# Cross-attention block in one launch: the context copy between the relus, a third buffer for the second sum, its store ahead of the probability transfers, and the last step's normalising on ScalarE

## The chip, the core and the metric

The kernel runs on one core of a Trainium2 chip. The metric is device time in microseconds of one launch, and the median of several runs counts. Five engines work side by side, each through its own instructions in order: TensorE (PE, with its weight loads as PEld), VectorE (DVE), ScalarE (ACT), GpSimd (POOL) and SyncE (SP), which here issues nearly all transfers. They wait for one another through semaphores, and a wait holds up whatever stands behind it on the same engine.

## What is computed

One block of cross attention in float32 over 128 sequences of 128 tokens, width 256, 16 heads of 16, feed-forward width 1024:

```python
q = (x @ Wq + bq)      # 16 heads; k and v likewise from ctx
scores = q k^T / 4, kept where j < i, else -1e30
attn = softmax(scores);  attn[row 0] = 0
x1  = layer_norm(x + (attn @ v) @ Wo + bo, ln1_g, ln1_b)
out = layer_norm(x1 + relu(x1 @ W1 + b1) @ W2 + b2, ln2_g, ln2_b)
```

## The kernel before

Sequences go in pairs: pair p holds sequences 2p and 2p+1, and there are 64 pairs (`NP`). All order is written out by hand; nothing is rescheduled. The first pairs have functions of their own (`third` to `sixth`), then `step(p)` runs for p = 7 to 63, and `behind(62)`, `behind(63)` and a written-out end finish the last pairs.

A step is a software pipeline over several pairs. In `step(p)` the following happens, by engine:

- PE: `weigh(p-2)` multiplies probabilities and values into PSUM bank 7 (tile `pc`, L494 and L504), `scores_both(p)` fills all eight banks (`pss`, L384), then come the queries (`pq`, L261), `attention_out(p-2)` (`po`, L523), keys and values (`pk`, `pv`), `second_by_seven(p-4)` (the second feed-forward product by seven products instead of eight; `py` in bank 6 and `pz` in bank 7, L817) and `hidden_by_seven(p-3)` (the first feed-forward product, chunks 0 to 3 by seven products, `phs`, L907, and chunks 4 to 7 plainly, `ph`, L946). The last step uses the plain `hidden` (L718) instead.
- ACT: `context(p-2)` copies `pc` into `cxT` (L516) and so frees bank 7; then come the exponentials by head (L783), the copies of queries, keys and values, `norm1`, `norm2` of pair p-5 (L602), and the relus that make `hT` (L936 in ordinary steps, L726 where `hidden` is used). In `hidden_by_seven` the relus go in the order 4, 5, 6, 7, 0, 1, 2, 3, all before the context copy of the following step.
- POOL: `combine_hidden(p-4)` makes four sums and differences `hS` of `hT` (L803 to L806) and needs all eight relus; then `add_bo`, `combine_normed` (`xS`, L874 to L877), the small steps of the norms (`ve`, `sd`, `nb`: L543, L544, L588), the multiplication of the exponentials by one over their sums (L434), `residual1` (L577, L580) and `finish(p-5)` (L616, L617: gain and offset of the second norm on `t2`).
- DVE: masks (L398, L762) and maxima (L766, L773) of the scores, `attention_sum`, statistics (L536, L537), transposes of 32 by 32 blocks of the probabilities (`turn`, L447) and of the normed rows (`tbx`, L682), the sum `t2` of `sum_of_seven(p-4)` (L846, L854), and the additions inside `hidden_by_seven` (L919 to L931).
- SP: `turn_x1` sends the normed rows through DRAM (L239, L242), `bring(p)` carries the transposed probabilities to their partitions (`pT`, L462, 16 transfers), `store(p-5)` writes the result (L625), `load_ahead` fetches inputs (L92, L99).

The tile `t2` lives from `sum_of_seven(p-4)` in one step to `store(p-5)` in the next; its pool `ffn` has two buffers, so a new `t2` waits until the store of the second-last one has read its buffer. In `step` the order on SP is `bring(p)` and then `store(p-5)`.

In the last step (p = 63) the normalising of pair 58 is done by `norm2_by_vector` on DVE (L610), the statistics of pair 59 close the step, and half of the probability transfers of pair 63 are issued by ACT in `behind(62)`.

Of the kernel before, what the change touches and what calls it, by code (L numbers as in the profile page):

```python
# [19 lines left out]
def tile_cross_attention_block(  # L20
# [346 lines left out]
    def scores_both(p):  # L367

        st = states[p]
        for hi in range(2):  # L370
            st["sps", hi] = [
                at_bank(r if hi else (6, 7, 4, 5)[r], f"pss{hi}_{p}_{r}") for r in range(NS)
            ]
            room(p, hi)
        one, two = (0, 1), (2, 3)
        for strips, hi, m in (
            (two, 0, 0), (one, 1, 0), (two, 0, 1), (one, 1, 1),
            (two, 1, 0), (two, 1, 1), (one, 0, 0), (one, 0, 1),
        ):
            n = P if hi else HP  # L380
            for s in range(2):
                for r in strips:
                    strip, first = slice(32 * r, 32 * r + 32), s * P
                    nc.tensor.matmul(  # L384
                        st["sps", hi][r][
                            s * HP : (s + 1) * HP, m * 2 * n : (m + 1) * 2 * n
                        ].rearrange("p (e j) -> p e j", e=2),
                        st["qT"][strip, m, first + hi * HP : first + hi * HP + HP],
                        st["kT"][strip, m, :, first : first + n],
                        start=True, stop=True,  # L390
                    )
# [49 lines left out]
    def turn(p, hi, t):  # L441

        st = states[p]
        if "tb" not in st:
            st["tb"] = wide(f"tb_{p}").rearrange("p (j n) -> p j n", j=NS)
        at = (t if hi else 2) * 256
        nc.vector.transpose(  # L447
            st["tb"][:, :, at : at + 256].rearrange("p j (n a) -> p n j a", a=32),
            st["sm", hi].rearrange("p h j -> p (h j)")[:, t * 1024 : (t + 1) * 1024].rearrange(
                "p (n j a) -> p n j a", j=NS, a=32  # L450
            ),
        )
# [61 lines left out]
    def context(p):  # L514
        pc = states[p].pop("pc").rearrange("p (u i) -> p u i", i=P)
        nc.scalar.copy(cxT.rearrange("p m s i -> p (m s) i")[:, :, 1:], pc[:, :, 1:])  # L516
# [75 lines left out]
    def scale_and_shift(p):  # L592

        st = states[p]
        deviation(p, 2)
        shift(p, 2)
# [6 lines left out]
                t2[:, s], t2[:, s], AF.Identity, bias=nb[:, s], scale=sd[:, s]  # L603
            )

    def norm2_by_vector(p):
        st = states[p]
        t2, mv, sd = st["t2"], st["mv", 2], st["sd", 2]
        for s in range(2):
            nc.vector.tensor_scalar(  # L610
                t2[:, s], t2[:, s], mv[:, s, 0:1], sd[:, s], ALU.subtract, ALU.mult
            )

    def finish(p):
        t2 = states[p]["t2"]
        nc.gpsimd.tensor_tensor(t2, t2, g2_r[:, None, :].to_broadcast([P, 2, D]), ALU.mult)  # L616
        nc.gpsimd.tensor_tensor(t2, t2, be2_r[:, None, :].to_broadcast([P, 2, D]), ALU.add)  # L617
# [126 lines left out]

    def second_sum(p):
        st = states[p]
        t2 = st["t2"] = ffn.tile([P, 2, D], F32, tag="t2", name=f"t2_{p}")
        nc.vector.tensor_tensor(
            t2, st.pop("py").rearrange("p (s d) -> p s d", s=2), st.pop("x1b"), ALU.add
        )  # L750
# [85 lines left out]
    def sum_of_seven(p):  # L836

        st = states[p]
        t2 = st["t2"] = ffn.tile([P, 2, D], F32, tag="t2", name=f"t2_{p}")
        t = t2.rearrange("p s (h d) -> p (s h) d", h=2)  # L840
        py, pz = st.pop("py"), st.pop("pz")
        x1b = st.pop("x1b").rearrange("p s (h d) -> p (s h) d", h=2)

        def add(to, of, at):
            n = to.shape[1]
            nc.vector.tensor_tensor(  # L846
                to, of, py[:, None, at * P : (at + 1) * P].to_broadcast([P, n, P]), ALU.add
            )

        add(t, x1b, 0)  # L850
        add(t[:, 1:], t[:, 1:], 1)
        add(t[:, 2:], t[:, 2:], 2)
        add(t[:, 1::2], t[:, 1::2], 3)
        nc.vector.tensor_tensor(  # L854
            t[:, :3], t[:, :3], pz[:, : 3 * P].rearrange("p (n d) -> p n d", d=P), ALU.add
        )
# [95 lines left out]
    def second_half(p, s):  # L952

        st = states[p]
        py = at_bank(6, f"py_{p}_{s}")
        for f in range(FC):
            nc.tensor.matmul(
                py[:, :D], st["hT"][:, f, s * P : (s + 1) * P], w2[:, f, :],
                start=(f == 0), stop=(f == FC - 1),
            )  # L960
        if s == 0:
            st["t2"] = ffn.tile([P, 2, D], F32, tag="t2", name=f"t2_{p}")
        nc.vector.tensor_tensor(st["t2"][:, s], py[:, :D], st["x1b"][:, s], ALU.add)

    warm = bank("warm")
# [365 lines left out]
    def hidden_by_seven(p):  # L1331

        h = Hidden(p - 3)
        h.run(1)
        h.run(6)
        h.keep()
        stack_values(p)
        h.u2()
        h.run(7)
        h.run(4)  # L1340
        h.u3()
        h.run(2)
        h.run(3)
        h.run(5)
        h.rest()
        norm2(p - 5)
        h.plain([4], 0)
        h.relu(4)
        h.plain([5], 1)
        h.relu(5)  # L1350
        h.plain([6], 2)
        h.relu(6)
        turn(p, 1, 1)
        h.plain([7], 0)
        h.relu(7)
        for f in range(2 * NI):
            h.relu(f)

    def step(p):
        last = p == NP - 1  # L1360
        weigh(p - 2)
        context(p - 2)
        scores_both(p)
        combine_hidden(p - 4, POOL_ALONE)
        add_bo(p - 1)
        if not last:
            combine_normed(p - 3)
            load_ahead(p)
        mask(p, 0, B)
        if last:  # L1370
            mask(p, 0, A)
        mask_high(p, A)
        exponential_by_head(p, 1, ONES, True)
        mask_high(p, B)
        exponential_by_head(p, 1, TWOS, True)
        if not last:
            mask(p, 0, A)
        low_maximum(p)
        if not last:
            exponential_by_head(p, 0, range(H), True)  # L1380
            queries(p + 1)
        attention_out(p - 2)
        attention_sum(p - 2)
        attention_stats(p - 2)
        shift(p - 2, 1)
        if last:
            values(p)
            values_out(p)
            stats(p - 5, states[p - 5]["t2"], 2)
            deviation(p - 5, 2)  # L1390
            norm1(p - 2)
            exponential_by_head(p, 0, range(H), True)
        else:
            norm1(p - 2)
            keys(p + 1)
            values(p)
        sums(p, 1, ONE)
        sums(p, 1, TWO)
        if p + 2 < NP:
            tokens(p + 2, "x")  # L1400
            tokens(p + 2, "c")
        if last:
            norm2_by_vector(p - 5)
            turn_x1(p - 2)
        else:
            stats(p - 5, states[p - 5]["t2"], 2)
            scale_and_shift(p - 5)
        turn(p, 1, 0)
        second_by_seven(p - 4)
        if not last:  # L1410
            sums(p, 0, ALL)
        residual1(p - 3)
        sum_of_seven(p - 4)
        if last:
            sums(p, 0, ALL)
        if not last:
            turn_x1(p - 2)
            spread_values(p)
            hidden_by_seven(p)
        else:  # L1420
            turn(p, 1, 1)
            hidden(p - 3, range(FC))
        turn(p, 0, 0)
        bring(p, nc.sync, LATE_FIRST[: len(EVERY) // (1 + last)])
        finish(p - 5)
        store(p - 5)
        if last:
            stats(p - 4, states[p - 4]["t2"], 2)
            scale_and_shift(p - 4)

    third()
    fourth()
# [8 lines left out]
    def behind(p):  # L1441

        weigh(p)
        context(p)
        if p == NP - 2:
            bring(p + 1, nc.scalar, LATE_FIRST[len(EVERY) // 2 :])
        combine_hidden(p - 2, VECTOR_ALONE)
        norm2(p - 3)
        finish(p - 3)
        store(p - 3)  # L1450
        second_by_seven(p - 2)
        attention_out(p)
        attention_sum(p)
        attention_stats(p)
        shift(p, 1)
        residual1(p - 1)
        sum_of_seven(p - 2)
        stats(p - 2, states[p - 2]["t2"], 2)
        scale_and_shift(p - 2)
        hidden(p - 1, range(FC), lambda f: norm1(p) if f == 0 else None)  # L1460
        turn_x1(p)
# [16 lines left out]
    store(p - 1)  # L1478

    st = states[NP - 1]  # L1480
    t2 = ffn.tile([P, 2, D], F32, tag="t2", name="t2_last")
    for s in range(2):
        py = at_bank(6 + s, f"py_last_{s}")
        for f in range(FC):
# [49 lines left out]
```

## Time and profile before

| | us |
|---|---|
| median of 3 runs | 1533.78 |
| lowest and highest run | 1531.72, 1533.82 |
| the profiled execution's own time | 1532.45 |
| its span, first to last instruction | 1529.5 |
| what lies around the span | 2.95 |

| engine | busy us | share of the span |
|---|---|---|
| PE | 1510.4 | 99% |
| PEld | 1368.7 | 89% |
| POOL | 1358.2 | 89% |
| DVE | 1294.3 | 85% |
| ACT | 1287.0 | 84% |

The mean granted clock of TensorE is 0.998 of full speed. Busy time says how full an engine is, not whether it is late: for that one asks what each engine waited for and when. In the rows of the timeline below, the first number is the start in microseconds, the second the duration, "xN" the number of instructions merged into the row, and the bracket the idle time of that engine just before and what ended it. A row with SPq or ACTq is the issuing of transfers by that engine's queue.

### The profile page before, as it was taken

To read this page: it belongs to the slowest core of one execution; us is meant where nothing else is said; L and a number is where in the kernel's file an instruction comes from. 1 tells how busy PE (TensorE), PEld (TensorE's weight loads), DVE (VectorE), ACT (ScalarE), POOL (GpSimd) and SP (SyncE) were. 2 spreads that over 40 slices of the span, in tenths; PEclk is the share of its full clock that TensorE was granted. 3 is DMA by queue.
4 is the path that set the end of the run, shared out by engine and by line. 5 is a ranking of instruction groups with operands and counts; after the bars stand their busy time and mean duration, and the time that the engine had idled before them with its cause. 6 is when DMAs were issued, how large, how long until landed. Compare 5 with 4: busy or idle time off the path is not lost.

```text
span 1529.5 us, 53568 instructions
## 1 busy us (share of the span) xinstructions
PE 1510.4 (99%) x18598; PEld 1368.7 (89%) x18598; DVE 1294.3 (85%) x2609; ACT 1287.0 (84%) x5269; POOL 1358.2 (89%) x1508
## 2 busy tenths in 40 slices
PE   8999999999999999999999999999999999999998
PEld 6788899989989989999999999999899999999987
DVE  7989788898888888888888888888888888888875
ACT  5568888988989889889889889889898898898852
POOL 7878889999999999999999999999999999999973
PEclk9999999999999999999999999999999999999999
DMA  8456656655656656656566566556565566564441
GB/s 196 91 117 149 135 136 138 136 135 135 150 132 141 136 133 140 144 138 139 129 138 145 135 138 137 135 135 151 131 141 132 137 139 148 133 141 114 107 115 49
DMA packets 415316, 204.60 MB, mean 134 GB/s; under 512 B 282449, under 2 KB 383057, under 8 KB 415057
## 3 DMA queue, kind: packets, MB, share of 16 engines
q1 hardware_dynamic: 412768, 199.34, 56.5%
q8 instruction: 158, 2.59, 0.8%
q10 hardware_dynamic: 2288, 1.85, 0.5%
q14 instruction: 102, 0.83, 0.2%
HBM read 70.26 MB, written 33.29 MB: 68 GB/s over the span
## 4 chain that ended last, share of the span: by engine, by line
PE 91%; DVE 4%; DMA 2%; POOL 1%; SPq 1%; issue 1%; ACT 1%; ACTq 0%; POOLq 0%; DVEq 0%
PE py L817 13%; PE ph L946 12%; PE phs L907 11%; PE pz L817 10%; PE pq L261 7%; PE pss L384 7%; PE po L523 7%; PE pv L301 7%; PE pk L261 7%; PE pc L504 4%; PE pc L494 2%; PE ph L718 2%; SPq L462 1%; DVE t L846 1%; POOL sm L434 1%
## 5 line engine op out<-in xcount | busy, mean ns | idle before, releaser
L783 ACT ACTIVATE sm<-pss,nmx 128x128 f32<-128x128 f32 x944 | 328.5, 404 | 107.0 <-DVE nmx L766 95.8
L434 POOL TENSOR_TENSOR sm<-sm,rs 128x1024 f32<-128x1024 f32 x192 | 362.2, 1901 | 5.6 <-DVE rs L433 5.6
L783 ACT ACTIVATE sm<-sm,nmx 128x64 f32<-128x64 f32 x944 | 313.8, 404 | 0.0
L447 DVE STREAM_TRANSPOSE tb<-sm 128x1024 f32<-128x1024 f32 x186 | 223.3, 1226 | 71.3 <-POOL sm L434 57.8
L783 ACT ACTIVATION_READ_ACCUMULATOR sm<-sm,nmx 128x1 f32 x912 | 235.5, 258 | 0.0
L783 ACT ACTIVATION_READ_ACCUMULATOR sm<-pss,nmx 128x1 f32 x912 | 222.6, 244 | 0.0
L946 PE MATMUL ph<-x1T,w 128*128 128x256 f32 x896 | 204.8, 382 | 3.3 <-DVE hT L919 3.3
L946 PEld LDWEIGHTS ph<-x1T,w 128*128 128x128 f32 x896 | 165.7, 191 | 25.8 <-DVE hT L919 3.7
L817 PE MATMUL py<-wt,hS 128*128 128x128 f32 x1440 | 170.7, 275 | 0.9 <-DVE hS L803 0.9
L817 PEld LDWEIGHTS py<-wt,hS 128*128 128x128 f32 x1440 | 165.6, 192 | 1.0 <-DVE hS L803 1.0
L766 DVE TENSOR_REDUCE nmx<-pss 128x4 f32<-128x512 f32 x236 | 150.5, 678 | 0.0
L936 ACT ACTIVATE hT<-ph,b1e_c 128x256 f32<-128x256 f32 x224 | 98.8, 465 | 44.1 <-PE ph L946 44.1
L398 DVE TENSOR_TENSOR sm<-pss,neg 128x256 f32<-128x256 f32 (+1 forms) x276 | 108.0, 433 | 32.4 <-PE pss L384 30.2
L291 ACT ACTIVATE kT<-pk,bkh,half 128x256 f32<-128x256 f32 x252 | 123.8, 610 | 4.0 <-PE pk L261 4.0
L261 PE MATMUL pq<-xT,wq 128*128 128x256 f32 x504 | 125.4, 392 | 0.0
L523 PE MATMUL po<-wo,cxT 128*128 128x256 f32 x512 | 121.3, 380 | 0.8 <-ACT cxT L516 0.8
L301 PE MATMUL pv<-wv,cT 128*128 128x256 f32 x512 | 121.0, 379 | 0.0
L261 PE MATMUL pk<-cT,wk 128*128 128x256 f32 x504 | 119.2, 379 | 0.0
L803 POOL TENSOR_TENSOR hS<-hT 128x512 f32<-128x512 f32 x57 | 72.6, 1274 | 50.4 <-ACT hT L936 50.2
L384 PE MATMUL pss<-kT,qT 32*64 32x256 f32 (+1 forms) x3840 | 112.7, 332 | 0.6 <-ACT hT L726 0.6
L523 PEld LDWEIGHTS po<-wo,cxT 128*128 128x128 f32 x512 | 96.9, 190 | 14.4 <-ACT cxT L516 1.3
L301 PEld LDWEIGHTS pv<-wv,cT 128*128 128x128 f32 x512 | 97.2, 190 | 13.2
(165 smaller groups left out, 3982.0 us busy)
## 6 DMA issues: line engine op xcount, KB each, us to landing
pT<-tb SPq DMA_DIRECT2D x976, 96.0 KB, 2.2
x1t<-tbx SPq DMA_DIRECT2D x252, 64.0 KB, 1.8
x1T<-x1t SPq DMA_DIRECT2D x63, 256.0 KB, 2.9
out_dram<-t SPq DMA_DIRECT2D x63, 256.0 KB, 2.6
xb<-in_x_dram SPq DMA_DIRECT2D x124, 128.0 KB, 3.8
cb<-in_ctx_dram SPq DMA_DIRECT2D x124, 128.0 KB, 3.9
x<-in_x_dram SPq DMA_DIRECT2D x31, 512.0 KB, 4.7
w<-in_L_xattn_W_dram SPq DMA_DIRECT2D x2, 1024.0 KB, 7.3
```

The source lines that it names most:

```text
L261: nc.tensor.matmul(ps[:, m * TP : (m + 1) * TP], w[:, k, m * P : (m + 1) * P], src[:, k, :], start=(k == 0), stop=(k == KC - 1),)
L291: nc.scalar.activation(st["kT"][:, m, e, :], pk[:, m * TP : (m + 1) * TP], AF.Identity, bias=bkh[:, m, e : e + 1], scale=half[:, e : e + 1],)
L301: nc.tensor.matmul(pv[:, s * D : (s + 1) * D], st["cT"][:, k, s * P : (s + 1) * P], wv[:, k, :], start=(k == 0), stop=(k == KC - 1),)
L384: nc.tensor.matmul(st["sps", hi][r][s * HP : (s + 1) * HP, m * 2 * n : (m + 1) * 2 * n].rearrange("p (e j) -> p e j", e=2), st["qT"][strip ...
L434: nc.gpsimd.tensor_tensor(sm[:, part, :], sm[:, part, :], rs[:, :, None].to_broadcast([P, part.stop - part.start, n]), ALU.mult,)
L447: nc.vector.transpose(st["tb"][:, :, at : at + 256].rearrange("p j (n a) -> p n j a", a=32), st["sm", hi].rearrange("p h j -> p (h j)")[:, ...
L523: nc.tensor.matmul(po[:, s * D : (s + 1) * D], cxT[:, k, s, :], wo[:, k, :], start=(k == 0), stop=(k == KC - 1),)
L766: nc.vector.tensor_reduce(st["nmx", 1][:, 4 * r : 4 * r + 4], st["sps", 1][r].rearrange("p (n j) -> p n j", j=P), AX.X, ALU.max, negate=True,)
L783: nc.scalar.activation(sm[:, h, :], src, AF.Exp, bias=nmx[:, h : h + 1], scale=1.0, **({"accum_out": st["su", hi][:, h : h + 1]} if summed ...
L817: nc.tensor.matmul(out, left(k), right(k), start=(k == 0), stop=(k == FC // 2 - 1))
L907: nc.tensor.matmul(ps[:, i * P : (i + 1) * P].rearrange("p (n a) -> p n a", a=32), left(i), right, start=True, stop=True,)
L946: nc.tensor.matmul(self.plains[f].rearrange("p (s i a) -> p s i a", s=2, a=32), w1[:, k, f * P : (f + 1) * P], self.x1T[:, :, :, k, :], st ...
```

## The change

Four things are changed; the arithmetic of the matmuls and their order on PE stay as they are.

1. `hidden_by_seven` issues the relus 0 and 1 only (after 4 to 7), and keeps the object under `states[p - 3]["rest"]`; the relus 2 and 3 are issued in the next step, behind `context`. On ACT the copy of the context so stands between relu 1 and relu 2, in the steps 8 to 63.
2. `t2` has three buffers instead of two.
3. In the steps 7 to 62 `finish(p-5)` and `store(p-5)` are written ahead of `bring(p)`, which puts the store ahead of the 16 probability transfers on SP.
4. In the last step `norm2_by_vector(58)` on DVE goes; instead `shift(58, 2)` makes `nb` on POOL, and `norm2(58)` on ACT, `finish(58)` on POOL and `store(58)` are placed in `behind(62)` after the context copy, ahead of the eight transfers that ACT issues. The statistics of pair 59 move from the end of the last step to behind `combine_hidden` in `behind(62)`.

```diff
-    def norm2_by_vector(p):
-        st = states[p]
-        t2, mv, sd = st["t2"], st["mv", 2], st["sd", 2]
-        for s in range(2):
-            nc.vector.tensor_scalar(
-                t2[:, s], t2[:, s], mv[:, s, 0:1], sd[:, s], ALU.subtract, ALU.mult
-            )
...
-        t2 = st["t2"] = ffn.tile([P, 2, D], F32, tag="t2", name=f"t2_{p}")
+        t2 = st["t2"] = ffn.tile([P, 2, D], F32, tag="t2", name=f"t2_{p}", bufs=3)
...
         h.plain([7], 0)
         h.relu(7)
-        for f in range(2 * NI):
+        for f in range(NI):
             h.relu(f)
+        states[p - 3]["rest"] = h
 
     def step(p):
         last = p == NP - 1
         weigh(p - 2)
         context(p - 2)
+        if p > 7:
+            for f in range(NI, 2 * NI):
+                states[p - 4]["rest"].relu(f)
         scores_both(p)
...
         if last:
-            norm2_by_vector(p - 5)
+            shift(p - 5, 2)
             turn_x1(p - 2)
...
         turn(p, 0, 0)
+        if not last:
+            finish(p - 5)
+            store(p - 5)
         bring(p, nc.sync, LATE_FIRST[: len(EVERY) // (1 + last)])
-        finish(p - 5)
-        store(p - 5)
-        if last:
-            stats(p - 4, states[p - 4]["t2"], 2)
-            scale_and_shift(p - 4)
...
         weigh(p)
         context(p)
         if p == NP - 2:
+            norm2(p - 4)
+            finish(p - 4)
+            store(p - 4)
             bring(p + 1, nc.scalar, LATE_FIRST[len(EVERY) // 2 :])
         combine_hidden(p - 2, VECTOR_ALONE)
+        if p == NP - 2:
+            stats(p - 3, states[p - 3]["t2"], 2)
+            scale_and_shift(p - 3)
         norm2(p - 3)
```

More of the change, by code (lines that the diff above doesn't have):

```diff
@@ L838, in sum_of_seven @@
         st = states[p]
-        t2 = st["t2"] = ffn.tile([P, 2, D], F32, tag="t2", name=f"t2_{p}")
+        t2 = st["t2"] = ffn.tile([P, 2, D], F32, tag="t2", name=f"t2_{p}", bufs=3)
         t = t2.rearrange("p s (h d) -> p (s h) d", h=2)
@@ L961, in second_half @@
         if s == 0:
-            st["t2"] = ffn.tile([P, 2, D], F32, tag="t2", name=f"t2_{p}")
+            st["t2"] = ffn.tile([P, 2, D], F32, tag="t2", name=f"t2_{p}", bufs=3)
         nc.vector.tensor_tensor(st["t2"][:, s], py[:, :D], st["x1b"][:, s], ALU.add)
@@ L1480, in tile_cross_attention_block @@
     st = states[NP - 1]
-    t2 = ffn.tile([P, 2, D], F32, tag="t2", name="t2_last")
+    t2 = ffn.tile([P, 2, D], F32, tag="t2", name="t2_last", bufs=3)
     for s in range(2):
```

## The prediction

> **What bounds the kernel now.** I read the page's busy times first, then the list of who waited for whom on PE, then the timeline at the two places that list points to, and one ordinary step.
>
> ```profile
> PE 1510.4 (99%) x18598; PEld 1368.7 (89%) x18598; DVE 1294.3 (85%) x2609; ACT 1287.0 (84%) x5269; POOL 1358.2 (89%) x1508
> ```
>
> Of a span of 1529.5 us PE is idle for 1529.5 - 1510.4 = 19 in all. A change that leaves its instructions alone can gain only where PE waits. The list of PE's waits (total, times, longest) says where that is:
>
> ```profile
> PE ph L946 <- DVE hT L919: 3.3, 1, 3.3
> ...
> PE pc L494 <- DVE t L854: 1.9, 1, 1.9
> ...
> PE ph L718 <- DMA x1T<-x1t: 1.2, 2, 0.8
> ```
>
> Each of the first two happens once, the third twice, so none belongs to the repeated step. An ordinary step begins with the product `pc`; PE's rows at two successive steps:
>
> ```profile
> 819.39 0.43 PE L494 MATMUL pc<-pT,vd 128*32 128x64 f32 x16
> ...
> 842.61 0.43 PE L494 MATMUL pc<-pT,vd 128*32 128x64 f32 x16
> ```
>
> The step is 842.61 - 819.39 = 23.22 us, and the windows view of another step shows PE busy for all of it at full clock (second row; columns: window, length, then busy time and instructions of PE, PEld, DVE, ACT, POOL, then granted clock, DMA share, GB/s):
>
> ```profile
> 188.62:192.02 3.40, 3.30 (x8) 2.52 (x8) 3.12 (x6) 0.47 (x1) 0.00 (x0) 0.50 0.31 77
> 192.26:215.48 23.22, 23.22 (x293) 21.26 (x292) 18.76 (x42) 20.71 (x88) 20.07 (x23) 1.00 0.64 148
> ```
>
> So nothing is to be had in the ordinary step. There are two places to gain: the 3.3 us early on, and the 1.9 near the end with a smaller one behind it.
>
> **Third buffer: step 8.** The early wait lies in step 8. The rows of its start, its stall and the next step's start on PE and PEld, then DVE and SP:
>
> ```profile
> 163.84 0.27 PEld L494 LDWEIGHTS pc<-pT,vd 128*32 128x32 f32 x16 [0.33 <-issue]
> ...
> 188.72 3.61 PE L946 MATMUL ph<-x1T,w 128*128 128x256 f32 x8 [3.32 <-DVE hT L919]
> ...
> 192.26 0.27 PEld L494 LDWEIGHTS pc<-pT,vd 128*32 128x32 f32 x16 [0.48 <-issue]
> ```
> ```profile
> 184.90 0.69 DVE L846 TENSOR_TENSOR t<-x1b,py 128x512 f32<-128x512 f32 x1 [5.41 <-DMA out_dram<-t]
> ```
> ```profile
> 168.75 11.69 SPq L462 DMA_DIRECT2D pT<-tb  x16
> 180.54 0.53 SPq L625 DMA_DIRECT2D out_dram<-t  x1
> ```
>
> Step 8 takes 192.26 - 163.84 = 28.42 us, 5.20 more than 23.22. The chain reads backwards: PE waits for the addition L919 that frees a PSUM bank; DVE is late there because the first sum into `t2` waited 5.41 us for the store of the tile that holds its buffer; that store was issued only at 180.54, behind 16 probability transfers that began at 168.75. With three buffers the sum takes a buffer whose store went out a step earlier, so DVE goes on at 184.90 - 5.41 = 179.49. What frees PE at 188.72 comes 5.41 sooner too, at 183.31, and PE wants it only at 188.72 - 3.32 = 185.40. The whole 5.20 us goes, in two parts: PE's idle 3.32 and the half clock behind it. The first windows row above has a granted clock of 0.50 for 3.40 us, which costs about 3.40 x 0.5 = 1.70; the two make 5.0 of the 5.20.
>
> [...]
>
> **The last step and behind it.** DVE, then POOL, then PE:
>
> ```profile
> 1460.03 3.88 DVE L610 TENSOR_SCALAR t<-t,mv,sd 128x256 f32<-128x256 f32 x2 [1.64 <-POOL sd L544]
> ...
> 1464.45 1.20 DVE L447 STREAM_TRANSPOSE tb<-sm 128x1024 f32<-128x1024 f32 x1
> ...
> 1467.83 0.55 DVE L854 TENSOR_TENSOR t<-t,pz 128x384 f32<-128x384 f32 x1
> ...
> 1470.57 1.25 DVE L447 STREAM_TRANSPOSE tb<-sm 128x1024 f32<-128x1024 f32 x1 [0.92 <-POOL sm L434]
> ...
> 1472.78 0.88 DVE L803 TENSOR_TENSOR hS<-hT 128x512 f32<-128x512 f32 x1
> ```
> ```profile
> 1459.96 3.80 POOL L434 TENSOR_TENSOR sm<-sm,rs 128x1024 f32<-128x1024 f32 x2
> ...
> 1465.12 1.27 POOL L580 TENSOR_TENSOR x1b<-x1b,be1b_r 128x512 f32<-128x512 f32 x1
> 1468.62 1.91 POOL L434 TENSOR_TENSOR sm<-sm,rs 128x1024 f32<-128x1024 f32 x1 [2.23 <-DVE rs L433]
> ```
> ```profile
> 1468.44 0.43 PE L494 MATMUL pc<-pT,vd 128*32 128x64 f32 x16 [1.89 <-DVE t L854]
> ...
> 1473.72 0.49 PE L817 MATMUL py<-wt,hS 128*128 128x128 f32 x2 [0.86 <-DVE hS L803]
> ...
> 1486.12 0.43 PE L494 MATMUL pc<-pT,vd 128*32 128x64 f32 x16
> ```
>
> `norm2_by_vector` holds DVE for 3.88 us after a wait of 1.64. Without it the turn at 1464.45 waits only for the first of the two POOL multiplications, 1459.96 + 1.90 = 1461.86, so it and all behind it come 1464.45 - 1461.9 = 2.5 us sooner; L854 ends near 1465.9 instead of 1468.38. PE wants bank 7 at 1468.44 - 1.89 = 1466.55, so the wait of 1.89 goes whole.
>
> The other wait is for `hS`. The third multiplication on POOL now finds its sums ready; POOL is free at 1465.12 + 1.27 = 1466.4, and the added `shift` (two small instructions, taken as 0.25 each from the 0.23 of the small `ve` in the row at 806.73 below) makes that 1466.9. It ends at 1468.8, the turn takes 1.25 to 1470.1; the statistics that stood between the turn's end, 1470.57 + 1.25 = 1471.82, and `hS` at 1472.78 are moved behind, so the first `hS` ends at 1470.1 + 0.88 = 1471.0. PE wants it at 1473.72 - 0.86 - 1.89 = 1470.97. I count the 0.86 gone but for about 0.2. Gain here: 1.89 + 0.86 - 0.2 = 2.5.
>
> What is late next? ACT:
>
> ```profile
> 1471.84 6.72 ACTq L462 DMA_DIRECT2D pT<-tb  x8
> 1478.68 1.09 ACT L602 ACTIVATE t<-t,nb,sd 128x256 f32<-128x256 f32 x2 [8.00 <-DMA pT<-tb]
> 1481.10 0.84 ACT L726 ACTIVATE hT<-ph,b1e_c 128x256 f32<-128x256 f32 x2 [1.32 <-issue]
> ```
>
> The new `norm2(58)`, 1.09 us as that of pair 59, stands ahead of the eight transfers on ACT. It falls between the context copy and the turn that the transfers wait for anyway, so they begin at 1470.1 and end near 1476.8. Queued behind are `norm2(59)` and the relus, which PE's earlier pace asks for near 1481.10 - 2.5 = 1478.6; ACT is free by 1477.9. The transfers land by about 1479 (2.2 us behind their issue, by the list of transfers below), PE uses them at 1486.12 - 2.5 = 1483.6. If that cover went, ACT's 1.09 would be paid. The 0.8 for `x1T` stays: it hangs on the last `po`, which moves as a whole.
>
> **The ordinary step.** The edits touch it 56 times, so 0.1 us a step would be 5.6. ACT, POOL, DVE and SP of one step:
>
> ```profile
> 819.87 1.70 ACT L936 ACTIVATE hT<-hT,b1e_c 128x256 f32<-128x256 f32 x4
> 821.47 0.56 ACT L516 COPY cxT<-pc 128x508 f32<-128x508 f32 x1
> 823.80 0.37 ACT L783 ACTIVATE sm<-pss,nmx 128x128 f32<-128x128 f32 x1 [1.77 <-DVE nmx L766]
> ```
> ```profile
> 806.73 0.23 POOL L543 TENSOR_SCALAR ve<-mv 128x2 f32<-128x2 f32 x1 [0.23 <-DVE rs L433]
> ...
> 819.54 1.29 POOL L617 TENSOR_TENSOR t<-t,be_r 128x512 f32<-128x512 f32 x1
> 821.65 1.28 POOL L803 TENSOR_TENSOR hS<-hT 128x512 f32<-128x512 f32 x1 [0.82 <-ACT hT L936]
> ```
> ```profile
> 812.39 0.69 DVE L846 TENSOR_TENSOR t<-x1b,py 128x512 f32<-128x512 f32 x1 [0.57 <-DMA out_dram<-t]
> ...
> 821.67 0.42 DVE L398 TENSOR_TENSOR sm<-pss,neg 128x256 f32<-128x256 f32 x1 [0.60 <-PE pss L384]
> ```
> ```profile
> 821.10 11.05 SPq L462 DMA_DIRECT2D pT<-tb  x16
> ```
> ```profile
> 809.14 2.84 PE L817 MATMUL py<-wt,hS 128*128 128x128 f32 x24
> ...
> 820.31 0.63 PE L504 MATMUL pc<-pT,vz 128*32 128x64 f32 x32
> ```
>
> *Copy between the relus.* The copy can start once `pc` ends, 820.31 + 0.63 = 820.94, some 0.5 us sooner than 821.47; bank 7 comes free sooner, which PE does not need, as its scores already run without a wait. The relus 2 and 3 (half of 1.70) follow it, so the last ends near 822.4 instead of 821.57: 0.85 later. Behind them ACT waits until 823.80 anyway: no cost there. Behind them on POOL is `hS`, 0.85 later; PE asks for it at 809.14 + 23.22 = 832.4, more than 10 us after 821.65, so that is covered. POOL's chain then runs late by 0.85 until its own wait of 0.23 takes some back: 0.62 for the multiplications and the turn behind them. On DVE that 0.62 meets the 0.57 that the third buffer takes away, so the sums start within 0.1 of today's time. The end of POOL's round, 819.54 + 1.29 + 0.62 = 821.45, still lies before the next `hS`, whose start PE and ACT set: nothing adds up from step to step. Cost zero; between nothing and, if the cover failed, all of 0.85 x 56.
>
> *Store ahead of the transfers.* SP now waits for `finish`, at 821.45 instead of the turn at 821.1, and issues the store (0.53) first: the 16 transfers start 0.9 later and end near 833. They are wanted at 842.61, so some 7 us of cover remain after landing, the 2.2 us of the page's list of transfers counted off:
>
> ```profile
> pT<-tb SPq DMA_DIRECT2D x976, 96.0 KB, 2.2
> ```
>
> Behind them SP's next transfers move by 0.35 only, since the store no longer follows them.
>
> **The sum.** 5.20 + 2.5 + 0 = 7.7. The profiled execution took 1532.45, and would take 1524.75. The three other runs have a mean of 1533.11 (median 1533.78); from there 1525.4, which I give.
>
> **The rivals.**
>
> *Slower: the late relus reach the scores.* If `hS` moves by more than 0.23 + 0.57 + 0.60 = 1.4 us, the slack in POOL's and DVE's rows above is used up, the masks at 821.67 come late, with them maxima, exponentials and the copies that free PE's banks, and PE waits in each of 56 steps. Beyond 1.4, each 0.14 costs 7.7 us, the whole gain. At twice my shift, 1.7, it is 0.3 x 56 = 16.8 lost, 9.1 net: about 1542. For it: POOL is 89% busy. Against it: my shift is 0.85, from rows. 7%.
>
> *The tail gives nothing*: ACT's queue, with `norm2(58)` and eight issues of 6.72 us, takes the place of DVE's 3.88. Gain 5.20: 1527.9. Against it: ACT idles 8.00 there. 10%.
>
> *The clock*: in the timed runs the half rate was mostly absent. Gain 7.7 - 1.7 = 6.0: 1527.1. 8%.
>
> *The third buffer does not help step 8*: SP is behind there, its transfers starting at 168.75, 4.9 after the step's start against 821.10 - 819.39 = 1.7 in an ordinary one, and another of its transfers holds PE up instead. Gain 2.5: 1530.6, no change that can be told. 6%.
>
> **How the numbers follow.** The forecast has the other 69%. About 0.2%, or 3 us, is what a measurement of this kernel can tell from no change. Faster by more: forecast, tail and clock, 0.87; within: 0.06; slower: 0.07. Low end: lowest run 1531.72 less all waits named, 5.20 + 1.89 + 0.86 + 0.8 = 8.75: 1523. High end: highest run 1533.82 less 5.20: 1528.6, say 1529. That leaves out the last two rivals' 13% and slower readings of the first.
>
> **What would show it.** Right: step 8 as long as the others and no clock of 0.50 after the start; L846 without a wait for the store; steps still 23.22; `pc` after the last step without its 1.89. Wrong: steps of 23.3 or more, PE waiting for relus, for `hS`, or for `pT`.

## The result, and the profile after

| | before | after |
|---|---|---|
| median, us | 1533.80 | 1522.77 |
| lowest to highest, 4 runs each | 1531.72 to 1534.00 | 1522.34 to 1526.56 |
| the profiled execution's own time | 1532.45 | 1522.34 |
| its span | 1529.5 | 1520.5 |

The ratio is 0.9937, with a 95% interval of 0.9919 to 0.9955: 11.0 us faster by the medians. The sum of the forecast was 7.7, and the time it named, 1525.4, lies 8.4 below the median of before. The measured median lies 0.2 below the range's low end. On a second chip the same kernel gave 1521.46 (1520.80 to 1522.04) against 1530.86: 0.9932, 0.9908 to 0.9957.

Busy times from the page of after; line numbers are 8 lower than before for what stands behind the removed function (L846 is L838, L946 is L938, L803 is L795).

```profile
span 1520.5 us, 53525 instructions
PE 1506.5 (99%) x18598; PEld 1359.2 (89%) x18598; DVE 1281.6 (84%) x2607; ACT 1295.0 (85%) x5271; POOL 1358.2 (89%) x1510
```

PE's idle time went from 19 to 1520.5 - 1506.5 = 14 us, but its busy time fell by 3.9 too, with the same 18598 matmuls. That part is no wait that a list could have shown. The list of PE's waits (total, times, longest) has lost `ph` for DVE, `pc` for L854 and `ph` for `x1T`, and has two new entries for `hS`, besides one of 0.5 for `pq`, which waits once for DVE's mask:

```profile
PE ptp L477 <- issue: 2.2, 1, 2.2
...
PE py L809 <- DVE hS L796: 0.5, 1, 0.5
...
PE py L809 <- DVE hS L797: 0.5, 1, 0.5
```

To see where the 9.0 us of span went I divided both traces at the first `pc` of each step (and of the two `behind`):

| stretch | before | after | difference | forecast |
|---|---|---|---|---|
| start-up, to the first `pc` | 28.46 | 30.42 | +1.96 | 0 |
| first `pc` to the end of step 8 | 163.79 | 158.36 | -5.43 | -5.20 |
| of which step 8 itself | 28.42 | 23.15 | -5.27 | -5.20 |
| 54 ordinary steps | 1254.12 | 1250.92 | -3.20 | 0 |
| the last step, to the `pc` of `behind(62)` | 22.05 | 19.90 | -2.15 | -1.89 |
| `behind(62)` | 17.68 | 18.21 | +0.53 | -0.66 |
| `behind(63)` and the end | 37.52 | 36.48 | -1.04 | 0 |

Together -9.33; behind the last matmul 0.4 comes back. Two of the rows are not the change's doing. The start-up took either about 28.5 or 30.2 to 30.9 in all profiled executions below, whatever the edit. Of the 1.96 between before and after, 0.55 is there before the first `pk` (6.51 against 5.96), and 1.40 lies in sixteen products `ptp`: in after they take 3.34 us, with a granted clock of 0.50 from 26.0 to 29.4 us; in before 1.94, with 1.00. The end took 36.5 to 36.9 where its wait for `x1T` happened to be absent (before with the third buffer alone: 36.48) and 37.5 to 37.9 where it was there.

**Step 8.** DVE, then PE and the windows view (window, length, busy time and instructions of PE, PEld, DVE, ACT, POOL, then granted clock, DMA share, GB/s):

```profile
181.70 0.63 DVE L838 TENSOR_TENSOR t<-x1b,py 128x512 f32<-128x512 f32 x1
```
```profile
185.04 3.81 PE L938 MATMUL ph<-x1T,w 128*128 128x256 f32 x16
188.78 0.43 PE L494 MATMUL pc<-pT,vd 128*32 128x64 f32 x16
```
```profile
185.00:188.50 3.50, 3.50 (x18) 2.82 (x17) 2.98 (x7) 3.22 (x9) 3.42 (x4) 1.00 0.82 137
```

The first sum carries no bracket: it waits for no store. The sixteen products `ph` run on without a gap, and the clock stays at 1.00 where it was 0.50. Both parts of the forecast's first term are there.

**An ordinary step.** PE and ACT, then the same scores of before:

```profile
814.42 0.43 PE L494 MATMUL pc<-pT,vd 128*32 128x64 f32 x16
...
815.90 1.62 PE L384 MATMUL pss<-kT,qT 32*64 32x128 f32 x64
816.03 0.58 ACT L516 COPY cxT<-pc 128x508 f32<-128x508 f32 x1 [0.24 <-PE pc L504]
...
816.70 0.76 DVE L398 TENSOR_TENSOR sm<-pss,neg 128x256 f32<-128x256 f32 x2 [0.54 <-PE pss L384]
...
833.92 0.82 ACT L324 COPY vd<-pv 64x256 f32<-64x256 f32 x2
834.79 2.46 PEld L938 LDWEIGHTS ph<-x1T,w 128*128 128x128 f32 x12 [0.33 <-ACT vd L324]
...
837.58 0.43 PE L494 MATMUL pc<-pT,vd 128*32 128x64 f32 x16
```
```profile
820.87 1.88 PE L384 MATMUL pss<-kT,qT 32*64 32x128 f32 x64
```

The 64 score products start 1.48 behind the step's start in both (820.87 - 819.39, 815.90 - 814.42) and take 1.62 instead of 1.88. The copy that frees bank 7 starts 1.61 behind it instead of 2.08. So the scores did wait for bank 7 before, by 0.26 a step. The single records of the trace show it: in before the weight load that waits for ACT starts at 822.08, 0.05 behind the end of the copy (821.47 + 0.56), and the last 14 of the 64 products start behind it, when all others have started; in after it starts at 816.67, 0.06 behind the copy's end, while the others still run. It stood in no list because other score products, issued ahead of the wait, still ran: in before the last of them starts at 822.06 and takes 0.37, and the first that waited starts at 822.09, so PE counts as busy throughout. But the step became only 837.58 - 814.42 = 23.16 against 23.22. What is late next is in PEld's list, of before and of after:

```profile
PEld ph L946 <- ACT vd L324: 0.5, 2, 0.3
```
```profile
PEld ph L938 <- ACT vd L324: 18.8, 56, 0.5
```

In every step PE now reaches the plain product of chunk 5, which goes to bank 1, before ACT has copied the values `vd` out of that bank. That copy hangs on ACT's chain, which did not move: it starts 19.50 behind the step's start, in before 19.49. Of the 0.26 gained, 0.20 is waited away there. (In a second profiled execution of after, further down, the step is 23.14, so the gain is 0.06 to 0.09 a step.)

**The tail.** DVE, POOL and PE in `behind(62)`:

```profile
1463.15 0.65 DVE L795 TENSOR_TENSOR hS<-hT 128x512 f32<-128x512 f32 x1
1463.72 1.76 DVE L796 TENSOR_TENSOR hS<-hT 128x512 f32<-128x512 f32 x1
1465.40 1.75 DVE L797 TENSOR_TENSOR hS<-hS,hT 128x512 f32<-128x512 f32 x1
1467.19 0.69 DVE L798 TENSOR_TENSOR hS<-hT,hS 128x512 f32<-128x512 f32 x1
```
```profile
1463.13 1.79 POOL L608 TENSOR_TENSOR t<-t,g_r 128x512 f32<-128x512 f32 x1
1465.01 1.60 POOL L609 TENSOR_TENSOR t<-t,be_r 128x512 f32<-128x512 f32 x1
```
```profile
1459.61 0.43 PE L494 MATMUL pc<-pT,vd 128*32 128x64 f32 x16
...
1463.87 1.14 PE L809 MATMUL py<-wt,hS 128*128 128x128 f32 x8
1465.53 1.16 PE L809 MATMUL py<-wt,hS 128*128 128x128 f32 x8 [0.52 <-DVE hS L796]
1467.21 1.05 PE L809 MATMUL py<-wt,hS 128*128 128x128 f32 x7 [0.52 <-DVE hS L797]
```

The `pc` at 1459.61 has lost its 1.89. But two of DVE's four `hS` take 1.76 and 1.75 instead of 0.65 to 0.69, each beside one of POOL's two instructions of `finish(58)`, which the change has put at this place, and PE waits for both: its groups of eight products start 1465.53 - 1463.87 = 1.66 and 1467.21 - 1465.53 = 1.68 after one another, where eight run in about 0.9 (24 take 2.84 in an ordinary step of before). That is some 1.5 lost.

### The profile page after: what moved, and what is told of

The parts are those of the page before. It is cut to its first block, busy times and chain, and to the rows that moved or that the text cites. A ratio compares the mean times of both kernels' runs of the same rounds, so it can differ in the third digit from the quotient of the medians.

```text
span 1520.5 us, 53525 instructions
## 1 busy us (share of the span) xinstructions
PE 1506.5 (99%) x18598; PEld 1359.2 (89%) x18598; DVE 1281.6 (84%) x2607; ACT 1295.0 (85%) x5271; POOL 1358.2 (89%) x1510
## 3 DMA queue, kind: packets, MB, share of 16 engines
q8 instruction: 158, 2.59, 0.8%
## 4 chain that ended last, share of the span: by engine, by line
PE 92%; DVE 3%; ACT 2%; POOL 1%; DMA 1%; SPq 1%; issue 1%; ACTq 0%; POOLq 0%; DVEq 0%
PE ph L938 13%; PE py L809 13%; PE phs L899 11%; PE pz L809 10%; PE pq L261 7%; PE po L523 7%; PE pv L301 7%; PE pk L261 6%; PE pss L384 6%; PE pc L504 4%; PE ph L710 3%; PE pc L494 2%; ACT sm L775 1%; SPq L462 1%; POOL sm L434 1%
## 5 line engine op out<-in xcount | busy, mean ns | idle before, releaser
L938 PE MATMUL ph<-x1T,w 128*128 128x256 f32 x896 | 213.8, 386 | 0.1
L938 PEld LDWEIGHTS ph<-x1T,w 128*128 128x128 f32 x896 | 161.3, 190 | 36.1 <-ACT vd L324 18.8
L795 POOL TENSOR_TENSOR hS<-hT 128x512 f32<-128x512 f32 x57 | 72.2, 1267 | 50.2 <-ACT hT L928 50.1
L261 PEld LDWEIGHTS pq<-xT,wq 128*128 128x128 f32 x504 | 90.7, 189 | 20.8 <-issue 9.8
```

The source lines that it names most:

```text
L261: nc.tensor.matmul(ps[:, m * TP : (m + 1) * TP], w[:, k, m * P : (m + 1) * P], src[:, k, :], start=(k == 0), stop=(k == KC - 1),)
L938: nc.tensor.matmul(self.plains[f].rearrange("p (s i a) -> p s i a", s=2, a=32), w1[:, k, f * P : (f + 1) * P], self.x1T[:, :, :, k, :], st ...
```

## The experiments

The theory after the result: the third buffer gives step 8, the early copy gives the ordinary steps, the tail gives 1.96 and loses 0.53 to `finish(58)` on POOL. The rivals: the ordinary steps gained by the buffer or by the store's place; the tail's loss is ACT's queue and not POOL.

**One part alone.** The first is before with the third buffer only (the same edit at all four places that make a `t2`; one is shown), the second before with the two late relus only, the third after without them.

```diff
-        t2 = st["t2"] = ffn.tile([P, 2, D], F32, tag="t2", name=f"t2_{p}")
+        t2 = st["t2"] = ffn.tile([P, 2, D], F32, tag="t2", name=f"t2_{p}", bufs=3)
```

> The kernel before with the third buffer for t2 alone. Theory (freed bank: the ordinary step got shorter because the earlier context copy frees bank 7 sooner for the scores): step 8 loses its extra 5.2 us, the ordinary steps stay at 23.22, so about 5 us faster than before. Rival (the third buffer or the store's place shortens the ordinary step, by taking DVE's wait of 0.57): the steps go to 23.16 as well, 53 x 0.06 = 3.3 more, about 8.5 faster.

```diff
-        for f in range(2 * NI):
+        for f in range(NI):
             h.relu(f)
+        states[p - 3]["rest"] = h
...
         context(p - 2)
+        if p > 7:
+            for f in range(NI, 2 * NI):
+                states[p - 4]["rest"].relu(f)
```

> The kernel before with the relus 2 and 3 behind the context copy alone. Freed bank: the products of the scores take about 0.26 us less in each step, the plain products wait about 0.19 for the copies of the values, the step is 23.16, and step 8 keeps its extra 5 us: 2 to 3.5 us faster than before. Rival: POOL's work comes 0.6 late without DVE's 0.57 to make it up, the masks are late, and the steps stay at 23.22 or grow; same or slower.

```diff
-        for f in range(NI):
+        for f in range(2 * NI):
             h.relu(f)
-        states[p - 3]["rest"] = h
...
-        if p > 7:
-            for f in range(NI, 2 * NI):
-                states[p - 4]["rest"].relu(f)
```

> The changed kernel with all eight relus ahead of the context copy again; third buffer, store and last step as changed. Freed bank: steps at 23.22, so 3.3 us slower than the changed kernel, about 6 faster than before. Rival: steps at 23.16 and no difference from the changed kernel.

| | median, us | ratio to before | step 8 | ordinary step (median of the 53 from step 10 on) | last | `behind(62)` |
|---|---|---|---|---|---|---|
| before | 1531.68 | | 28.42 | 23.222 | 22.05 | 17.68 |
| buffer alone | 1527.58 | 0.9970 (0.9956 to 0.9984) | 23.22 | 23.221 | 22.04 | 17.68 |
| copy alone | 1526.97 | 0.9969 (0.9955 to 0.9984) | 27.02 | 23.134 | 21.89 | 17.67 |
| after without the copy | 1525.92 | 0.9959 (0.9945 to 0.9972) | 23.73 | 23.221 | 20.09 | 18.12 |
| after | 1522.77 | 0.9937 (0.9919 to 0.9955) | 23.15 | 23.161 | 19.90 | 18.21 |

(Medians are those of the runs that went together; after's has its own before, 1533.80.) The parts separate cleanly. The buffer cures step 8 and leaves the ordinary step at 23.221. (The 23.73 in the row without the copy does not hang on the copy: two other kernels with the buffer have 23.7 too, and after itself has 23.15 and 23.13 in its two profiled executions.) Its group of first sums (busy, mean ns, then idle before them and its releaser) shows no DMA any more, where before had 32.9 us of waiting for stores:

```profile
L846 DVE TENSOR_TENSOR t<-x1b,py 128x512 f32<-128x512 f32 x60 | 41.1, 685 | 12.6 <-PE py L817 12.6
```
```profile
L846 DVE TENSOR_TENSOR t<-x1b,py 128x512 f32<-128x512 f32 x60 | 41.2, 686 | 39.6 <-DMA out_dram<-t 32.9 <-PE pz L817 3.3 <-PE py L817 3.2
```

The copy alone shortens the ordinary steps and brings the new wait with it, while the stall of step 8 stays. With it comes the half clock: 0.50 from 190.99 to 194.40, this time partly in step 9, which takes 23.95. The waits of PE and PEld of that kernel:

```profile
PE ph L946 <- DVE hT L919: 2.8, 1, 2.8
```
```profile
PEld ph L946 <- ACT vd L324: 18.2, 56, 0.6
```

**The store's place, and the rival that said slower.** Two kernels from after: the store behind the transfers again; and all four in-place relus behind the copy, twice the forecast's shift, at which the rival wanted PE to wait in every step.

```diff
         turn(p, 0, 0)
+        bring(p, nc.sync, LATE_FIRST[: len(EVERY) // (1 + last)])
         if not last:
             finish(p - 5)
             store(p - 5)
-        bring(p, nc.sync, LATE_FIRST[: len(EVERY) // (1 + last)])
```

> The changed kernel with the store behind the probability transfers on SP again. Theory: the place of the store moves nothing that PE waits for; steps stay at 23.16 and step 8 at 23.2, span within 1 us of 1520.5 apart from the start. Rival: the store's place was part of what shortened the steps or of what cured step 8; steps at 23.22 or step 8 longer by some us.

```diff
-        for f in range(NI):
-            h.relu(f)
         states[p - 3]["rest"] = h
...
-            for f in range(NI, 2 * NI):
+            for f in range(2 * NI):
                 states[p - 4]["rest"].relu(f)
```

> The changed kernel with all four in-place relus behind the context copy, so that hS on POOL starts another 0.85 us later, 1.65 later than in the kernel before. If the slack of 1.4 us that the prediction added up from POOL's and DVE's rows is right, it is overrun by about 0.25, the masks come late and the steps lengthen by 0.2 to 0.3, in all 10 to 15 us slower than the changed kernel. Rival: there is more cover than that, and the steps stay at 23.16.

One run each: 1522.85 and 1525.0. With the store behind, the ordinary step is 23.161 and `behind(62)` 18.19, as in after: its place is worth nothing that this one execution shows, as forecast. With all four relus behind, the step is 23.164; start-up (30.92) and the wait for `x1T` (end 37.69) explain most of the 2.2 that the span is longer. The rival's loss of 16.8 did not come, but its mechanism is there. The step's start and the masks in this kernel, and in the lists of waits after's `tb` and this kernel's:

```profile
815.24 0.43 PE L494 MATMUL pc<-pT,vd 128*32 128x64 f32 x16
```
```profile
817.52 0.76 DVE L398 TENSOR_TENSOR sm<-pss,neg 128x256 f32<-128x256 f32 x2
```
```profile
DVE tb L447 <- POOL sm L434: 90.7, 47, 3.1
```
```profile
DVE tb L447 <- POOL sm L434: 141.3, 53, 3.9
```

DVE waits longer for POOL ahead of the turn, and comes to the masks with no wait left (after: 0.54), at the same 2.28 behind the step's start. So the whole shift of some 1.7 us is just covered.

**The tail's loss.** `finish(58)` and its store go behind `shift(62, 1)`, past DVE's `hS`, with ACT's `norm2(58)` and transfers left where they are. If POOL is the cause, `behind(62)` falls by about 1.5; if ACT's queue is, nothing changes.

```diff
             norm2(p - 4)
-            finish(p - 4)
-            store(p - 4)
             bring(p + 1, nc.scalar, LATE_FIRST[len(EVERY) // 2 :])
...
         shift(p, 1)
+        if p == NP - 2:
+            finish(p - 4)
+            store(p - 4)
```

> The changed kernel with finish and store of pair 58 put off until after the first norm of pair 62, so that POOL does no work on whole tiles while DVE makes hS. Theory: in the changed kernel two of the hS instructions on DVE took 1.76 instead of 0.69 us because POOL's finish ran beside them; without it they take 0.7 and PE's two waits of 0.5 go, the stretch behind the last step is 16.8 instead of 18.2, about 1.4 us faster. Rival: DVE is slow there for another reason, or the put-off finish delays the relus: no gain.

1519.94 (1518.14 to 1520.85), ratio 0.9914 (0.9894 to 0.9933). `behind(62)` is 16.62, 1.59 less than after. DVE, then PE:

```profile
1463.52 0.68 DVE L796 TENSOR_TENSOR hS<-hT 128x512 f32<-128x512 f32 x1
1464.12 0.68 DVE L797 TENSOR_TENSOR hS<-hS,hT 128x512 f32<-128x512 f32 x1
```
```profile
1463.70 2.90 PE L809 MATMUL py<-wt,hS 128*128 128x128 f32 x24
```

The sums are back at 0.68 and the 24 products run without a gap. It was POOL.

**The wait for bank 1.** If the ordinary step now ends on that wait, then doing chunk 6 (bank 2) ahead of chunk 5 (bank 1) should give the 0.20 back in every step. The second kernel adds the late `finish`.

```diff
-        h.plain([5], 1)
-        h.relu(5)
         h.plain([6], 2)
         h.relu(6)
+        h.plain([5], 1)
+        h.relu(5)
```

> The changed kernel with the plain products of chunk 6 (bank 2) ahead of those of chunk 5 (bank 1). Theory: in the changed kernel PE gives back 0.19 us of the 0.26 per step because bank 1 is wanted before the copies of the values have left it; with the order swapped that wait goes, the step is near 22.97, 54 steps gain about 10 us: near 1512.5. Rival: ScalarE's or VectorE's chain holds the step in another place too, the wait only moves, and the time stays within 2 us of the changed kernel.

> Both the swapped plain products (chunk 6 ahead of chunk 5) and the put-off finish on the changed kernel. Theory: steps at 22.97 with occasional longer ones in the second half as the swap alone had, and 1.4 us less behind the last step: 3 to 4 us faster than the changed kernel, up to 10 if the long steps stay away. Rival: the long steps come more often; same as the changed kernel.

Measured 1521.36 (1519.16 to 1522.82), ratio 0.9925 (0.9899 to 0.9951), and 1521.38 (1518.00 to 1522.07), 0.9923 (0.9904 to 0.9942). The forecast of the step was right, 22.965, that of the time was not: from about 880 us on nearly every second step is 0.6 to 1.3 us longer, the others still 22.96. PE in such a step of the first kernel:

```profile
1109.52 1.11 PE L384 MATMUL pss<-kT,qT 32*64 32x128 f32 x31
1111.34 1.09 PE L384 MATMUL pss<-kT,qT 32*64 32x256 f32 x33 [0.70 <-issue]
```

PE stands still in the middle of the scores and waits for nothing that the profile knows ("issue"). The order of the chunks took one semaphore instruction out of PE's program: 639 instructions a step by the trace, 640 in before and after. The page has a row for an instruction queue (the first column is the number of transfers, the second MB; here of after):

```profile
q8 instruction: 158, 2.59, 0.8%
```

That is 2.59 MB / 158 = 16.4 KB each; the trace's own records have 16384 bytes for every one. PE has 40641 instructions in the trace of after. My estimate from these numbers, if the transfers are PE's program: one instruction is 2.59 MB / 40641 = 64 bytes, a block is 16384 / 64 = 256 of them, and a step of 640 is two and a half blocks: the borders between blocks lie at the same instructions in every second step. With 639 they wander. Theory: PE stalls when a border comes to lie in the scores. Rival: it is the new order of the chunks, or some heat or clock effect late in the run.

**One empty instruction.** `second_by_seven` already fills its products up with empty PE instructions, by a number that is the last argument of `product`. One more on the last product brings the step of 639 back to 640 and that of after to 641.

```diff
-        product(pz[:, P : 2 * P], lambda k: hs[:, 3, k], weights(1, 1), 6)
+        product(pz[:, P : 2 * P], lambda k: hs[:, 3, k], weights(1, 1), 7)
```

On the kernel with both edits, swap and late `finish`:

> The swapped plain products and the put-off finish, and one more empty instruction for PE in each product of the second feed-forward layer (49 instead of 48 a step). With the swap PE issues 639 instructions a step instead of 640, one wait fewer; from about 880 us on every second step was some 0.7 us longer. Theory: PE's instructions come in blocks of 16384 bytes, 640 instructions are two and a half of them, and with 639 the block border wanders until it falls into the dense products; with 640 again all steps are 22.97, and the whole is 10 us faster than the changed kernel, near 1511. Rival: the long steps come from transfers or from POOL and stay; no gain over the swap without the pad.

On after:

> The changed kernel with one more empty instruction for PE a step, 641 instead of 640, nothing else. Theory of the wandering block border: the first steps are 23.16 as before, and later some steps are longer by some tenths of a microsecond, every second one in a row of steps. Rival: one empty instruction changes nothing; all steps 23.16.

And after again beside them:

> The changed kernel once more, for comparison on the same chip: steps of 23.16, the stretch behind the last step 18.2, about 0.6% faster than before.

| | instructions a step | time, us | ratio | ordinary step: median, mean |
|---|---|---|---|---|
| after again | 640 | 1521.46 (4 runs) | 0.9932 (0.9908 to 0.9957) | 23.136, 23.139 |
| after, one empty instruction more | 641 | 1538.31 (1 run) | | 23.140, 23.481 |
| swap and late `finish` | 639 | 1521.38 (4 runs) | 0.9923 (0.9904 to 0.9942) | 22.965, 23.137 |
| the same, one more | 640 | 1510.33 (5 runs) | 0.9859 (0.9834 to 0.9884) | 22.964, 22.969 |

An instruction that does nothing costs one kernel about 17 us (one run; in its trace the 54 steps are together 18.1 longer than in that of after again) and saves the other about 10 (by the ratios; its 54 steps are 8.9 shorter). The chunks' order and the lateness in the run are out: at 641 the order is after's, and the long steps come in the middle of the run, mostly from 447 to 1063 us. The clock is out too: the mean granted clock is 0.999 in the profiled execution at 641, and 0.998 in the three others. PE's waits and two stalls, two steps apart, at 641:

```profile
PE pss L384 <- issue: 11.8, 11, 1.5
```
```profile
727.17 1.57 PE L384 MATMUL pss<-kT,qT 32*64 32x128 f32 x61
729.83 0.43 PE L384 MATMUL pss<-kT,qT 32*64 32x128 f32 x3 [1.09 <-issue]
...
774.74 1.57 PE L384 MATMUL pss<-kT,qT 32*64 32x128 f32 x60
777.26 0.43 PE L384 MATMUL pss<-kT,qT 32*64 32x128 f32 x4 [0.95 <-issue]
```

The gap moves from behind the 61st score product to behind the 60th: one product, that is two instructions, in two steps, as a border must at 641. Counted through the whole program the sign is sharper still. From step 9 on, all 15 gaps of over 0.55 us between the starts of neighbouring matmuls in the steps at 641 stand at the same place modulo 256 (instruction 11714, 12994, ... 30914: remainder 194), and all 13 such gaps in the two kernels with 639 at remainder 195, where the weight load just ahead, remainder 194, comes late already. So in all three kernels the first late instruction is number 194 of 256, as it must be if the stalls are at block borders. At 640 this place falls near products 42, 170 and 273 of one step (counted from its first `pc`) and 106 and 217 of the next, for good. At 641 it wanders down through products 164 to 149 (the first queries and the scores) while there are gaps of this size; at 639 up through 123 to 135.

Why a border hurts there and not near product 106, which is a score product too, the same traces show: it goes with how quickly PE uses up the block ahead of the border. Most of a step is slow products, but the 96 `pc` and the 64 scores, 320 instructions, take 1.48 + 1.62 = 3.1 us, so a block that lies in them is gone quickly. From step 9 on, in all kernels of this case, about 1700 blocks took over 3.5 us, and none was followed by a stall of over 0.2; in the kernels with 640 the quickest block takes 4.26. At 639 and 641, 54 blocks were used up in under 3.5 us (down to 2.14), and 39 of them were followed by such a stall. That the next block has then not come in yet is a guess of mine, which no row shown here tests; why 15 of the 54 go without stays open.

The last kernel, with after's edits, the swapped chunks, the late `finish` and the empty instruction, beats both: 0.9859 of before, against after's 0.9932 on the same chip.

## Why the prediction was right, and where it was not

*Step 8, -5.20: right in size and in both parts.* -5.27, from the idle time and from the half clock; the buffer alone does it. The rival of another transfer holding PE up did not come. The clock rival stays open for the runs of before without a profile; both profiled executions that have the stall, before and the copy alone, have the half rate too, and its cost went with the stall.

*The ordinary step, cost zero: wrong, in the gainful direction.* The step that failed is "bank 7 comes free sooner, which PE does not need, as its scores already run without a wait". They ran without an idle row, which is not the same. With it fails the premise that a gain lies only where the list of PE's waits shows one. The rows quoted there could not show it; comparing the 1.88 of the row `pss` with what 64 such products take unhindered, here 1.62, would have. The term measured -0.06 times 54, or -3.2: -0.26 gross, 0.20 of it returned at bank 1. So "steps still 23.22" was the wrong sign to look for. It is this term that carries the time below the range.

*The tail, -2.5: right in its first part, wrong in its second.* The 1.89 went (1.96 by the traces, with the scores' 0.19 counted off the last step's 2.15). The 0.86 for the first `hS`, "gone but for about 0.2", went, but waits for the second and third came in its place: measured against the kernel with the late `finish`, whose `behind(62)` is 16.62, before loses 1.06 in this stretch and after 1.59. The step that failed is the cost of `finish(58)` on POOL, which the working put at nothing: it took the first sum at 0.88, from rows where POOL did something else, and asked only when that first one was ready. With `finish(58)` moved away, the whole 0.86 and a little more is had.

*The store ahead of the transfers, zero: right*, by the kernel that puts it back.

*The late relus, zero with 1.4 us of slack: right*, and twice the shift still costs nothing, though DVE's wait at the masks is then gone; the rival had the mechanism, and its threshold of 1.4 was too low by 0.3 at least.

*The 0.8 for `x1T` "stays": neither.* It was absent in the profiled execution of after, and 1.0 and 1.1 in two other kernels' (all four relus behind; swap and late `finish`); what decides it is not shown.

Together: the forecast had -7.7; the traces show -5.43, -3.20 and -1.62 (last step and `behind(62)`), -10.2, without what varies of itself. Errors of +0.9 in the tail and -3.2 in the steps partly met, and that was luck.

## What to carry to other kernels

A stall among small matmuls need not show as idle time: here 64 score products took 1.88 us instead of 1.62 with no idle row. Compare how long such a group takes with what the same group takes where nothing holds it, and before a step is called full, follow the copies that free its banks. When an instruction is moved on POOL, look what DVE does beside it at the new place, and cost it there: here two sums of 0.68 took 1.76 and 1.75. Where a loop is written out in full, count PE's instructions per step: here 640 went without the long gaps, 639 and 641 did not, and one empty instruction cost one kernel about 17 us and gave another about 10. Then look how long PE takes for the 256 instructions ahead of each place where it stands still; here under 3.5 us was the sign of danger, with 39 stalls in 54 such blocks.

## What the hardware showed that was not expected

*DVE's sums ended only behind the POOL instructions beside them.* POOL's L608 ends at 1463.13 + 1.79 = 1464.92; DVE's L796, begun at 1463.72, ends at 1465.48, 0.56 behind it. POOL's L609 ends at 1466.61; L797 ends at 1467.15, 0.54 behind that. L608 itself is some 0.5 longer than the 1.29 of an ordinary `finish` instruction (L617 of before), which is about as long as L795 ran beside it. Where POOL's `finish(58)` is moved away, the two sums take 0.68 each. The rows look as if each engine waited until the other was through and then ran about its normal time; that is my reading of these four instructions, and what held them no row shows.

*The place of PE's long gaps hung on the number of its instructions.* At 641 instructions a step there was up to 1.5 us of standing still at one place in every second step over a long stretch, in all about 17 us (one run); at 639 the long steps were 0.6 to 1.3 us longer; at 640 the mean step is within 0.005 of the median (23.139 against 23.136, 22.969 against 22.964). The gaps lie multiples of 256 instructions apart, and 16384 bytes a transfer at my estimate of 64 an instruction are 256 too. That the borders of these transfers cost next to nothing at 640 and much at 639 and 641 is the reading that fits; no row shows PE waiting for one.
